# A rare loop moved ahead of the slots' layout, and the loads and the bias of a count-matrix layer reordered, in a four-layer graph network

## The chip, the cores and the metric

The kernel runs on one core of a Trainium2 chip. The core has five engines: TensorE (PE, with PEld for its weight loads), VectorE (DVE), ScalarE (ACT), GpSimd (POOL) and SyncE (SP, which mostly issues transfers). Transfers are issued from SP, ACT or POOL and are moved by 16 DMA engines. The metric is the device time of one execution in microseconds (us), the median of several. Fewer is better.

## The reference: what is computed

The input is a graph with N = 3125 nodes of 128 features and E = 100000 edges sorted by destination. Each edge has a relation (of 500), a type (of 8) and three attributes; each node has one of four types. Four layers follow one another, each with a residual and a layer norm:

```python
x = _layernorm(x + _L0_gnn_ref(x, ...))   # attention with relations
x = _layernorm(x + _L1_gnn_ref(x, ...))   # mean over the neighbours, two products
x = _layernorm(x + _L2_gnn_ref(x, ...))   # attention with an edge bias
x = _layernorm(x + _L3_gnn_ref(x, ...))   # attention with node and edge types
```

Layer 0 is a softmax over each node's incoming edges; the logits are `leaky(hP1[dst] + hP2[src] + zP3[edge_type]) @ y_w`, with eight heads. Layer 1 is

```python
summed = segment_sum(x[col], row); agg = summed / max(deg, 1)[:, None]
h = relu(agg @ W1.T + b1); return h @ W2.T + b2
```

Layer 2 adds `edge_attr @ We` (four heads) to its logits; this sum over the three attributes is the `bias` of the kernel.

## The kernel before, in words

The nodes are sorted by their number of edges and cut into 25 tiles of 128. Tile t gives every node CAP[t] slots, one for an edge, so that there are NS = 821 slots in each of 128 partitions. A node with more edges than slots is rare; its remaining edges are left to a loop, whose trips are computed on the chip (`rounds`, L476 to 488) and which makes none for these inputs.

The span has these stages.

- **Edge tables and order, 0 to 142 us.** The tables h_tab and z_tab, the table of edges and the sorted order of the nodes are made.
- **Slots' layout, L497 to 532, 142 to 193 us, in a pool of its own (`srcp`).** POOL gathers the 25 blocks of edge records into pay_sb (L503). DVE writes from them the slots' sources (srcx), masks and relations (rel). SP stores pay_sb into pay_tab (L504), for later layers, and PE, ACT and SP transpose the relations and store them as rel_tab (L529 to 532).
- **Layer 0, L885 on, 197 to 2528 us.** Its pools (`l0` and others) are opened where srcp was closed. First come m, l and nosum (L891 to 896), set to constants by DVE, and a store of nosum's zeros over sums_tab (2.4 MB, L898). Then the rare loop: `behind(wp, behind0)` calls the function at L773, which makes cur and left (L776 to 778), reads rounds into a register of every engine (L779) and runs the loop (L780). Its body `behind0` goes over all 25 tiles. After it, a planner places every step of the main work (gathers of hs rows by srcx, matmuls, softmax, sums and counts) by costs and due times; the order on DVE, ACT and PE is then as written. POOL's order (x and hs gathers) and SP's are set by the scheduler. The counts of edges between tiles are stored as c_tab, for layer 1.
- **Layer 1, L1438 to 1571, 2530 to 2730 us.** u1 (2.46 MB, L1443) holds layer 0's result times W1 in three parts of bf16. A branch (L1456, `tc.If`) deals with rare cases and is not taken here. POOL gathers 25 blocks of xn (the nodes' residual rows, in tile order). DVE makes `degrow` by way of a transpose and a transfer (L1526 to 1530). SP loads `pays` (L1536), DVE copies idx3 (L1537) and makes `bias` in twelve instructions (L1540). Then the loop over c, seven parts of 512 columns, loads the count part cs (3.2 MB, two buffers, L1546). PE adds b1 times degrow (L1549) and 75 matmuls (L1552) into y_ps. DVE and ACT make hT of it (L1554, L1555). For each of the part's four tiles, PE multiplies by W2 (o_ps, L1559), DVE adds b2 to xn (L1560), forms y and the layer norm, and PE multiplies by the next layer's weights. The scheduler may put an instruction of later source lines ahead of earlier ones on an engine, if their data allow it.
- **Layers 2 and 3, 2746 to 5236 us.** Gathers of key and value rows on POOL, products and reductions on DVE. Each has a rare loop of the same kind ahead of it.

The two places where the source order matters for the change are these:

```python
def behind(pool, body):                                   # L773
    cur = pool.tile([P, NT], F32, name="cur", bufs=1)
    V.tensor_add(cur, od.start, caps)                     # L776
    ...
    trips = nc.values_load(rounds, min_val=0, max_val=E)  # L779
    with tc.For_i(0, trips, 1):                           # L780
```

Of the kernel before, what the change touches and what calls it, by code (L numbers as in the profile page):

```python
# [86 lines left out]
def tile_gnn(ctx, tc, a, out):  # L87
# [409 lines left out]
    with tc.tile_pool(name="srcp", bufs=1) as sp, tc.tile_pool(name="srcq", bufs=2, space=PSUM) as ps:  # L497

        pay_sb = sp.tile([P, NS, PW], I32, name="pay_sb")
        start_i = sp.tile([P, NT], I32, name="start_i")  # L500
        V.tensor_copy(start_i, od.start)
        for t in range(NT):
            gather(pay_sb[:, OFF[t]:OFF[t + 1], :].rearrange("p s w -> p (s w)"), edge_tab, start_i[:, t:t + 1])  # L503
        nc.sync.dma_start(pay_tab, pay_sb.rearrange("p s w -> p (s w)"))  # L504
        srcs = sp.tile([P, NS], I32, name="srcs")
        for t in range(NT):
            sl = slice(OFF[t], OFF[t + 1])
            V.tensor_copy(srcx[:, sl], pay_sb[:, sl, 0])
            live = sp.tile([P, max(CAP)], F32, name="live", bufs=2)
            V.tensor_scalar(live[:, :CAP[t]], slotid[:, :CAP[t]], od.deg[:, t:t + 1], None, op0=OP.is_lt)  # L510
            V.tensor_scalar(mask[:, sl], live[:, :CAP[t]], -NEG, NEG, op0=OP.mult, op1=OP.add)
            V.scalar_tensor_tensor(rel[:, sl], pay_sb[:, sl, 1], float(-PADREL), live[:, :CAP[t]],
                                   op0=OP.add, op1=OP.mult)
            V.scalar_tensor_tensor(srcs[:, sl], pay_sb[:, sl, 0], float(-NP), live[:, :CAP[t]],
                                   op0=OP.add, op1=OP.mult)
        V.tensor_scalar(rel, rel, float(PADREL), None, op0=OP.add)
        V.tensor_scalar(srcs, srcs, float(NP), None, op0=OP.add)
        digit = sp.tile([P, NS], I32, name="digit")
        V.tensor_scalar(digit, srcs, 127, None, op0=OP.bitwise_and)
        V.tensor_scalar(srclo, digit, 1.0, None, op0=OP.add)  # L520
        V.tensor_scalar(digit, srcs, 7, None, op0=OP.arith_shift_right)
        V.tensor_copy(srchi, digit)

        relf = sp.tile([P, NS], F32, name="relf")
        V.tensor_copy(relf, rel)
        for o in range(0, NS, P):
            n = min(P, NS - o)
            rps = ps.tile([P, P], F32, name="rps")
            T.transpose(rps[:n], relf[:, o:o + n], ident)  # L529
            r16 = sp.tile([P, P], F16, name="r16", bufs=2)  # L530
            A.activation(r16[:n], rps[:n], AF.Copy)
            nc.sync.dma_start(rel_tab[o:o + n], r16[:n])


# [350 lines left out]

    with tc.tile_pool(name="l0", bufs=2) as wp, tc.tile_pool(name="l0s", bufs=1) as sp, \
# [4 lines left out]
        m = sp.tile([P, NT, H], F32, name="m")  # L891
        V.memset(m, LOW)
        l = sp.tile([P, NT, H], F32, name="l")
        V.memset(l, 0.0)
        nosum = sp.tile([P, D + R], F32, name="nosum")
        V.memset(nosum, 0.0)
        sums_at = sums_tab.rearrange("(t p) d -> t p d", p=P)
        nc.sync.dma_start(sums_tab.rearrange("(t p) d -> p t d", p=P),  # L898
                          nosum.unsqueeze(1).to_broadcast([P, NT, D + R]))

        def sums_of(t):
            az = wp.tile([P, D + R], F32, name="az", bufs=4)
            nc.sync.dma_start(az, sums_at[t])
            return az[:, :D], az[:, D:], az

        def own(t):
            x = wp.tile([P, D], F32, name="x", bufs=5)
            G.memset(x, 0.0)
            gather(x, a["x"], od.ids(t), bounds_check=N - 1, oob_is_err=False)
            return x  # L910

        def prologue(x):

            yield from misc.take()
            tp = ps1.tile([P, P], F32, name="tp", tag="misc")
            T.transpose(tp, x, ident)
            yield 3
            xT = wp.tile([P, P], F32, name="xT", bufs=1)
            A.activation(xT, tp, AF.Copy)
            yield 3  # L920
            pw = ps1.tile([P, D + HC + H], F32, name="pw", tag="misc")
            T.matmul(pw, xT, w0, start=True, stop=True)
            yield 3
            hw = wp.tile([P, D + HC + H], F32, name="hw", bufs=3)
            A.activation(hw, pw, AF.Copy)
            hq = wp.tile([P, 3, D], BF16, name="hq", bufs=3)
            A.activation(hq[:, 0, :], pw[:, :D], AF.Copy)
            misc.give()
            yield 3
            hrest = wp.tile([P, D], F32, name="hrest", bufs=1)  # L930
            V.tensor_sub(hrest, hw[:, :D], hq[:, 0, :])
            yield 3
            A.activation(hq[:, 1, :], hrest, AF.Copy)
            yield 3
            V.tensor_sub(hq[:, 2, :], hrest, hq[:, 1, :])
            return hw, hq

        def argument(hq, k):

            pre = ps.tile([P, 4, P], F32, name="pre")  # L940
            for i in range(3):
                T.matmul(pre[:, :k], hq[:, i, :], identb.unsqueeze(1).to_broadcast([P, k, P]), start=(i == 0),
                         stop=False)
            return pre

        def through(pre, hs, s0, k):
            for s in range(k):
                T.matmul(pre[:, s, :], hs[:, s0 + s, :D], ident, start=False, stop=(s == k - 1))  # L948

        def logits(low, k, lg_ps):  # L950
            for s in range(k):
                T.matmul(lg_ps[:, s, :], low[:, s, :], yw8, start=True, stop=True)  # L952

        def halves(v, n, last=None):

            while n > 2:
                k = n // 2
                V.tensor_add(v[:, :k], v[:, :k], v[:, n - k:n])
                n -= k
                yield 2.5  # L960
            if n == 2:
                V.tensor_add(v[:, 0] if last is None else last, v[:, 0], v[:, 1])
                yield 2.5

        def spread(ac, hs, ex, n):

            val = hs[:, :n, D:2 * D]
            valh = val.rearrange("p s (h d) -> p s h d", h=H)
            V.tensor_tensor(valh, valh, ex.unsqueeze(3).to_broadcast([P, n, H, D // H]), op=OP.mult)
            yield 2.5  # L970
            yield from halves(hs[:, :, D:2 * D], n)

        def z_rows(hs, s0, k, rl):
            zs = wp.tile([P, 4, HC + R], F32, name="zs", bufs=3)
            for s in range(k):
                gather(zs[:, s, :], z_tab, rl[:, s0 + s:s0 + s + 1])
            return zs

        def with_z(hs, s0, k, zs):
            V.tensor_add(hs[:, s0:s0 + k], hs[:, s0:s0 + k], zs[:, :k, :HC])  # L980

        def z_sums(za, zs, w):
            if len(zs) > 1:
                k = w - 4
                V.tensor_add(zs[0][:, :k, HC:], zs[0][:, :k, HC:], zs[1][:, :k, HC:])
                yield 2.5
            yield from halves(zs[0][:, :, HC:], min(w, 4))
            V.tensor_add(za, za, zs[0][:, 0, HC:])

        def drawn(steps):  # L990
            while True:
                try:
                    next(steps)
                except StopIteration as e:
                    return e.value

        up = count_up(cp, ps1.tile([P, 2 * P], BF16, name="c_up"))
        lg_at = ps1.tile([P, 2, 3 * W, H], F32, name="lg")
        misc = Room(1)

        def behind0(t, pl, mk, rl):
            _, hq = drawn(prologue(own(t)))
            ac, za, az = sums_of(t)
            lg_ps = lg_at[:, 0, :W]
            hs = wp.tile([P, W, HC], F32, name="hs", bufs=8)
            zss = []
            for s in range(W):
                gather(hs[:, s, :], h_tab, pl[:, s, 0:1])
            for s0 in range(0, W, 4):
                zss.append(z_rows(hs, s0, 4, rl))  # L1010
                with_z(hs, s0, 4, zss[-1])
            drawn(z_sums(za, zss, W))
            for s0 in range(0, W, 4):
                pre = argument(hq, 4)
                through(pre, hs, s0, 4)
                low = wp.tile([P, 4, P], F32, name="low")
                A.activation(low, pre, AF.Relu)
                logits(low, 4, lg_ps[:, s0:s0 + 4])
# [1098 lines left out]
```

## Time and profile before

| what | value |
|---|---|
| median of three runs | 5248.34 us (5230.04 to 5253.61) |
| the profiled execution | 5237.84 us, of which the span is 5236.0 us |
| mean granted PE clock in it | 0.674 of full speed |
| busy share: PE, DVE, ACT, POOL | 42%, 56%, 19%, 52% |
| POOL's gathers, hs / kv of layer 2 / kv of layer 3 | 830.3 / 781.6 / 852.5 us busy, 821 each |
| DMA | 482.23 MB, mean 92 GB/s |
| the three loads or stores that the change moves | sums_tab 2.4 MB, pays 2463 KB, cs 3200 KB each |

The page gives the busy time of each engine, the same in 40 slices of 131 us each (each digit is tenths), and the chain of work that ended last. In the timeline a row holds the start, the duration, the engine, the line, the operation and its output and input; in brackets stands how long the engine was idle before it and what released it. "SPq" and "POOLq" are the sequencers' own rows: issues of transfers, semaphores, branches.

### The profile page before, as it was taken

The page shows a single profiled execution, that of the slowest core. Times are in us where ns is not written, and L with a number is a line of the kernel's source. Part 1 is how long each engine was busy: PE and PEld are TensorE (multiplying, and loading weights), DVE is VectorE, ACT ScalarE, POOL GpSimd, SP SyncE. Part 2 cuts the span into 40 slices and gives each one's busy share as a digit, 9 for nine tenths or more (in the row PEclk, how much of TensorE's full clock was granted, in tenths as well). Part 3 has the DMA queues.
Part 4 walks back from the last instruction along what each step waited for, and adds up shares of the span by engine and source line. Part 5 has one row for each costly group of instructions (what it writes and reads, how often), then busy time and mean ns, then how long its engine had stood idle before and what let it go on. Part 6 is the DMA issues. An engine that isn't in the chain of part 4 may idle for free. (4 is left out here: it accounts for less than half of the span.)

```text
span 5236.0 us, 41120 instructions
## 1 busy us (share of the span) xinstructions
PE 2202.4 (42%) x12631; PEld 1450.8 (28%) x12631; DVE 2941.6 (56%) x6913; ACT 999.5 (19%) x2533; POOL 2723.1 (52%) x2802
## 2 busy tenths in 40 slices
PE   7176777786765777778480022322333000000000
PEld 5154455554544555555230011111111000000000
DVE  8355565665564665665524456556665455554555
ACT  1132233232322333332110011111112000000000
POOL 0524445435334443442217766666662777777774
PEclk9588788788777787888695555555556555555555
DMA  3422233323223222232343333333332333333331
GB/s 83 123 57 78 75 87 87 83 64 91 71 61 89 79 81 79 80 89 73 142 150 105 97 99 104 112 109 114 114 113 86 105 98 93 93 92 93 92 93 50
DMA packets 211921, 482.23 MB, mean 92 GB/s; under 512 B 60713, under 2 KB 110684, under 8 KB 207049
## 3 DMA queue, kind: packets, MB, share of 16 engines
q0 software_dynamic: 130688, 377.49, 25.5%
q1 hardware_dynamic: 80968, 101.69, 6.2%
q8 instruction: 106, 1.74, 0.1%
q14 instruction: 159, 1.30, 0.1%
HBM read 408.43 MB, written 70.63 MB: 91 GB/s over the span
## 5 line engine op out<-in xcount | busy, mean ns | idle before, releaser
L101 POOL DMA_INDIRECT hs<-h_tab,srcx x821 | 830.3, 1011 | 795.3 <-issue 448.8
L101 POOL DMA_INDIRECT kv<-ktv_tab,idx x821 | 852.5, 1038 | 283.2 <-issue 278.4
L101 POOL DMA_INDIRECT kv<-kv_tab,srcx x821 | 781.6, 952 | 357.5 <-issue 254.9
L1593 DVE TENSOR_TENSOR kv<-kv,qp 128x1024 f32<-128x1024 f32 (+4 forms) x228 | 253.2, 1110 | 687.2 <-DMA kv<-ktv_tab,idx 452.4
L1247 PE MATMUL zps<-oh,zq 128*128 128x512 bf16 x1472 | 415.5, 429 | 83.8 <-ACT zT L1252 40.2
L1604 DVE TENSOR_REDUCE u<-kv 128x128 f32<-128x1024 f32 (+4 forms) x228 | 383.8, 1683 | 25.1 <-issue 24.0
L1317 PE MATMUL t_ps<-zw,zT 128*128 128x136 f32 x1472 | 261.4, 315 | 147.2 <-DVE hs L1326 118.0
L1326 DVE TENSOR_TENSOR hs<-hs,t_ps 128x408 f32<-128x408 f32 (+1 forms) x276 | 145.1, 526 | 253.9 <-remote 165.5
L948 PEld LDWEIGHTS pre<-ident,hs 128*128 128x128 f32 x1642 | 244.8, 211 | 137.7 <-issue 132.7
L567 DVE TENSOR_TENSOR c_ohs<-c_ends,c_up 128x1024 bf16<-128x1024 bf16 (+3 forms) x196 | 115.9, 593 | 296.4 <-remote 207.1
L1317 PEld LDWEIGHTS t_ps<-zw,zT 128*128 128x128 f32 x1472 | 217.6, 213 | 170.6 <-issue 79.6
L1596 DVE TENSOR_REDUCE lg<-kv 128x32 f32<-128x1024 f32 (+5 forms) x228 | 251.8, 1104 | 21.7 <-issue 21.4
L948 PE MATMUL pre<-ident,hs 128*128 128x128 f32 x1642 | 250.6, 295 | 29.8 <-issue 28.5
L1600 DVE TENSOR_TENSOR kv<-kv,ex 128x1024 f32<-128x1024 f32 (+4 forms) x228 | 251.3, 1102 | 12.0 <-issue 11.9
L952 PEld LDWEIGHTS lg<-yw,low 128*128 128x128 f32 x1642 | 242.1, 222 | 42.3 <-issue 36.5
L952 PE MATMUL lg<-yw,low 128*128 128x8 f32 x1642 | 238.3, 269 | 28.9 <-issue 27.4
L677 ACT ACTIVATE c_oha<-c_oha,srclo 128x50 bf16<-128x50 bf16 (+2 forms) x821 | 213.0, 347 | 183.0 <-DVE c_oha L567 104.1
L1247 PEld LDWEIGHTS <-zq 128*128 128x128 bf16 x1472 | 157.2, 112 | 265.4 <-issue 163.6
L750 ACT ACTIVATE c_sb<-c_ps 128x512 bf16<-128x512 f32 (+1 forms) x175 | 96.3, 550 | 637.8 <-remote 332.0
L836 PE MATMUL tp<-ident,an 128*128 128x128 f32 x25 | 10.8, 434 | 480.7 <-remote 428.5
L1287 PE MATMUL pre<-zT,zw 128*128 128x512 f32 x368 | 209.3, 652 | 1.9 <-issue 1.8
L567 DVE TENSOR_TENSOR c_ohb<-c_digb,c_up 128x1024 bf16<-128x1024 bf16 (+4 forms) x123 | 73.3, 602 | 241.9 <-remote 112.5
(418 smaller groups left out, 4807.7 us busy)
## 6 DMA issues: line engine op xcount, KB each, us to landing
rb<-rel_tab SPq DMA_DIRECT2D x92, 256.0 KB
c_tab<-c_sb SPq DMA_DIRECT2D x25, 768.0 KB
cs<-c_tab SPq DMA_DIRECT2D x6, 3200.0 KB
hs<-h_tab,srcx POOLq DMA_INDIRECT x821
kv<-kv_tab,srcx POOLq DMA_INDIRECT x821
kv<-ktv_tab,idx POOLq DMA_INDIRECT x821
h_tab<-h SPq DMA_DIRECT2D x25, 132.0 KB
kv_tab<-kv SPq DMA_DIRECT2D x25, 128.0 KB
```

The lines of the kernel that those rows point to most:

```text
L101: return G.indirect_dma_start(out=dst, out_offset=None, in_=table, in_offset=indirect(idx), **kw)
L567: V.tensor_tensor(to[:, i // 2:i // 2 + k, :, :w], nums[:, i:i + k * w] .rearrange("p (b w) -> p b w", w=w).unsqueeze(2).to_broadcast([P, ...
L677: A.activation(oha[:, s // 2, 0, :, s % 2], oha[:, s // 2, 1, :, s % 2], AF.Copy, scale=srclo[:, o:o + 1])
L948: T.matmul(pre[:, s, :], hs[:, s0 + s, :D], ident, start=False, stop=(s == k - 1))
L952: T.matmul(lg_ps[:, s, :], low[:, s, :], yw8, start=True, stop=True)
L1247: T.matmul(zps, zq[:, i, 2 * R * k2:2 * R * (k2 + 1)], k.hot[i][:, cols], start=(i + k2 == 0), stop=(i == NK - 1 and k2 == 1))
L1287: T.matmul(pre[:, :n], zw[:, :D], k.zT[:, s0 * P:(s0 + n) * P], start=False, stop=False)
L1317: T.matmul(t_ps[:, s, :], k.zT[:, (s0 + s) * P:(s0 + s + 1) * P], zw[:, D:], start=True, stop=True)
L1593: V.tensor_mul(k, k, qp.unsqueeze(1).to_broadcast([P, n, D]))
L1596: V.tensor_reduce(lg, kv[:, :n, :D].rearrange("p s (h d) -> p s h d", h=heads), AX.X, OP.add)
L1600: V.tensor_tensor(v, v, ex.unsqueeze(3).to_broadcast([P, n, heads, D // heads]), op=OP.mult)
L1604: V.tensor_reduce(u, kv[:, :n, D:].rearrange("p s d -> p d s"), AX.X, OP.add)
```

## The change

It has two parts. In layer 0, m, l, nosum, the store over sums_tab, the functions that the loop's body calls (unchanged) and the loop itself now stand ahead of the slots' layout. The loop's tiles are in pools of its own (`b0`, `b0p`, `b0q`), closed before `srcp` is opened; m, l and nosum are in the pool `slots`, which is open from the start.

```diff
     rel_tab = dram.tile([-(-NS // P) * P, P], F16, name="rel_tab")
-    with tc.tile_pool(name="srcp", bufs=1) as sp, tc.tile_pool(name="srcq", bufs=2, space=PSUM) as ps:
-        pay_sb = sp.tile([P, NS, PW], I32, name="pay_sb")
...
+    m = slots.tile([P, NT, H], F32, name="m")
+    V.memset(m, LOW)
+    l = slots.tile([P, NT, H], F32, name="l")
+    V.memset(l, 0.0)
+    nosum = slots.tile([P, D + R], F32, name="nosum")
+    V.memset(nosum, 0.0)
+    sums_at = sums_tab.rearrange("(t p) d -> t p d", p=P)
+    nc.sync.dma_start(sums_tab.rearrange("(t p) d -> p t d", p=P),
+                      nosum.unsqueeze(1).to_broadcast([P, NT, D + R]))
+    with tc.tile_pool(name="b0", bufs=2) as wp, tc.tile_pool(name="b0p", bufs=2, space=PSUM) as ps, \
+            tc.tile_pool(name="b0q", bufs=1, space=PSUM) as ps1:
+        lg_at = ps1.tile([P, 2, 3 * W, H], F32, name="lg")
+        misc = Room(1)
+        behind(wp, behind0)
+
+    with tc.tile_pool(name="srcp", bufs=1) as sp, tc.tile_pool(name="srcq", bufs=2, space=PSUM) as ps:
+        pay_sb = sp.tile([P, NS, PW], I32, name="pay_sb")
...
     with tc.tile_pool(name="l0", bufs=2) as wp, tc.tile_pool(name="l0s", bufs=1) as sp, \
...
-        m = sp.tile([P, NT, H], F32, name="m")
...
         up = count_up(cp, ps1.tile([P, 2 * P], BF16, name="c_up"))
         lg_at = ps1.tile([P, 2, 3 * W, H], F32, name="lg")
         misc = Room(1)
-        behind(wp, behind0)
```

In layer 1, the loads of the first two count parts are issued by the scalar engine, and the load of pays, idx3 and the twelve bias instructions stand in the loop behind the matmuls of part 1.

```diff
-        with tc.tile_pool(name="l1pay", bufs=1) as pp:
-            pays = pp.tile([P, NS, PW], I32, name="pays")
-            nc.sync.dma_start(pays.rearrange("p s w -> p (s w)"), pay_tab)
-            V.tensor_copy(idx3, pays[:, :, 2])
-            ...
         for c in range(NCW):
             w = min(CW, NP - c * CW)
             cs = wp.tile([P, NT, CW], BF16, name="cs")
-            nc.sync.dma_start(cs[:, :, :w], ...)
+            load_by = nc.scalar if c < 2 else nc.sync
+            load_by.dma_start(cs[:, :, :w], ...)
             y_ps = ps1.tile([P, CW], F32, name="y_ps", bufs=2)
 
             T.matmul(y_ps[:, :w], b1, degrow[:, c * CW:c * CW + w], start=True, stop=False)
             for t in range(NT):
                 for k in range(3):
                     T.matmul(y_ps[:, :w], u1[:, t, k, :], cs[:, t, :w], start=False, stop=(t == NT - 1 and k == 2))
+            if c == 1:
+                with tc.tile_pool(name="l1pay", bufs=1) as pp:
+                    pays = pp.tile([P, NS, PW], I32, name="pays")
+                    nc.sync.dma_start(pays.rearrange("p s w -> p (s w)"), pay_tab)
+                    V.tensor_copy(idx3, pays[:, :, 2])
+                    for h in range(H2):
+                        for k in range(3):
+                            V.scalar_tensor_tensor(bias[:, :, h], pays.bitcast(F32)[:, :, 3 + k],
+                                                   we[:, k * H2 + h:k * H2 + h + 1], mask if k == 0 else bias[:, :, h],
+                                                   op0=OP.mult, op1=OP.add)
             hT = wp.tile([P, CW], F32, name="hT")
```

## The prediction on record

> **What bounds the kernel now.** I read the page first: the slices and the chain of work that ended last.
>
> ```profile
> POOL 0524445435334443442217766666662777777774
> POOL 15%; issue 8%; DVE 0%; another core or an unknown queue 0%; POOLq 0%; DMA 0%; DVEq 0%
> ```
>
> No engine is busy throughout, and the chain that ended last is POOL's row gathers of the last layer. That chain covers a quarter of the span, so it says nothing about the two places that the change touches: the start of layer 0 (142 to 300 us) and layer 1 (2530 to 2730 us). For these I took the table by stretches. Columns after the time: PE, PEld, DVE, ACT, POOL busy, granted PE clock, DMA share, GB/s.
>
> ```profile
> 197.00:298.00 101.00, 12.52 (x61) 7.75 (x62) 16.88 (x32) 20.12 (x64) 70.76 (x78) 0.52 0.39 106
> 298.00:340.00 42.00, 39.66 (x272) 27.80 (x272) 29.43 (x75) 11.77 (x24) 0.00 (x0) 0.93 0.08 20
> 2572.00:2602.00 30.00, 21.18 (x85) 9.04 (x84) 22.01 (x19) 0.63 (x1) 0.00 (x0) 0.78 0.48 194
> 2624.00:2730.00 106.00, 100.74 (x487) 47.97 (x485) 34.99 (x153) 19.00 (x69) 20.45 (x21) 0.99 0.41 147
> ```
>
> The reader should see two things. From 197 to 298 us only POOL is busy: 78 gathers at about 1.25 us (0.95 busy and 0.30 between) take the 100 us, and the other engines start in earnest at 298. So layer 0 begins when POOL begins, and a shift of POOL's first gather shifts the layer. From 2624 on PE is busy 100.7 of 106 us, so layer 1 ends a fixed time after PE's first free run. Then the timeline at the rare loop (L780, no trip here):
>
> ```profile
> 192.94 0.19 DVE L776 TENSOR_TENSOR cur<-start_d,caps 128x25 f32<-128x25 f32 x1 [3.20 <-DMA rel_tab<-r]
> 196.94 0.20 POOL L908 MEMSET x<- 128x128 f32 x1 [21.41 <-SPq L780]
> 197.66 0.95 POOL L101 DMA_INDIRECT hs<-h_tab,srcx  x1 [0.53 <-issue]
> 198.72 0.18 DVE L633 SCALAR_TENSOR_TENSOR crowd<-c_pre,crowd 128x25 f32<-128x25 f32 x1 [5.50 <-issue]
> ```
>
> POOL stands 21.4 us at the loop; its last gather of pay_sb ended at 175.5. Next, the timeline at the head of layer 1:
>
> ```profile
> 2552.94 0.33 SPq L1536 DMA_DIRECT2D pays<-pay_tab  x1
> 2553.37 0.85 SPq L1530 DMA_DIRECT2D degrow<-dT  x1
> 2554.27 1.42 SPq L1546 DMA_DIRECT2D cs<-c_tab  x2
> ...
> 2562.72 3.78 PE L1549 MATMUL y_ps<-degrow,b 1*128 1x512 f32 x4 [19.18 <-DMA degrow<-dT]
> ...
> 2571.50 1.01 PE L1552 MATMUL y_ps<-cs,u 128*128 128x512 bf16 x2 [5.01 <-DMA cs<-c_tab]
> ...
> 2593.31 6.45 DVE L1540 SCALAR_TENSOR_TENSOR bias<-pays,we,bias 128x821 f32<-128x821 f32 x4
> 2599.68 0.68 DVE L1554 TENSOR_TENSOR hT<-y_ps,sums 128x512 f32<-128x512 f32 x1
> ```
> ```profile
> 2601.08 0.80 PE L1559 MATMUL o_ps<-w2T,hT 128*128 128x128 f32 x2 [8.82 <-ACT hT L1555]
> ```
>
> PE gets its first count part at 2571.5, has finished part 0 at 2591.9, and then stands 8.8 us, because hT of part 0 is queued on DVE behind idx3 (2579.5) and twelve bias instructions (2580.3 to 2599.6).
>
> **Part A, the loop ahead of the slots' layout.** Removed: the barrier at 189.6 to 198.7. Of it, POOL loses 4.3 us (the last rel_tab store lands near 192.6, POOL is out at 196.9), DVE 5.7 (192.94 to 198.72). Added: the same barrier before the first pay_sb gather, now at 144.39. The loop reads rounds, ready today at 146.7 behind 25 small DVE instructions, a reduction, a transpose and two more reductions; without the memsets of l and nosum among them, some 0.4 us earlier. From the register load to DVE's first instruction behind the loop today takes 198.57 - 193.01 = 5.6 us. start_i (0.2 us) and the gather's start (1.1 us after start_i today) follow: 146.3 + 5.6 + 0.2 + 1.1 = 153.2, a delay of 9 us. The store of zeros into sums_tab (2.4 MB, issued 146.71, moving until about 156) would hold the loop to some 157 if it stays where it is: delay 12 to 13. I expect it early, since its tile is no longer in layer 0's memory. Queued behind the delayed gathers: the 25 gathers themselves, DVE's 100 small slot instructions, the pay_tab store, seven transposes, seven rel_tab stores and SP's rb loads behind these. All move by 9, so the last rel_tab store lands near 201.6.
>
> Where a loss turns to a gain is what POOL waits for then. Its first gather of layer 0 writes into memory that overlaps pay_sb's pool. Today's row for the nearest case is L776 above: a small tile in layer 0's pool waited 3.2 us for the last rel_tab store, although that store doesn't read it, so a new pool waits for the whole old one. By this row POOL starts at 201.9, **5 us later** than 196.9 (8 later with sums_tab in the way). The other end: POOL waits only for pay_sb's readers, which end at about 185.4 + 9 and need no barrier; then it starts near 194.5 or, with its indices alone (181 + 9), at 190: **2.5 to 7 us earlier**; with a loop shorter than today's, 12 earlier. I take +5. What this costs DVE is covered: counting waits at most 1 us longer (198.72 to about 199.6), and DVE is idle for 84 of the 101 us that follow. Hoisted memsets (three at 0.23 us) are worth under 1 us.
>
> **Part B, layer 1.** Removed from SP's queue: two issues (1.42 us together) and, more, their place behind pays. SP issued the last weight at 2541.2 and then stood until 2552.6 for memory that the branch at L1456 holds; pays, degrow and cs came out in one burst. On ACT, which is idle from 2543 to 2600 (0.6 us busy in the stretch above), the loads can go out at 2530.7 (before ACT's branch) or 2539 (behind it). Cost on ACT: 2 x 0.7 us beside nothing.
>
> Landing: cs is 128 packets of 25,600 B of some 0.98 us on 16 engines, so a part alone takes 7.9 us. Sent with u1 (2.46 MB until 2540 today), cs0 lands near 2545. But w2, b2 and the three weights are 128 small packets each, 8 per engine, and stand on SP's ring beside ACT's; if rings take turns by packet, as the gathers' 4,096 B packets and the 25,600 B ones do from 2560 to 2579 (xn's additions on DVE wait 29.4 us for gathers there), each small packet waits about 1 us for a large one until cs1 is through, near 2553. PE transposes w2 ahead of dT (2542.3 and 2543.1 today), and degrow follows. So the first matmul of part 0 comes not at 2546 but near 2558, against 2571.5: 13 us early, bounded by 2548 (nothing in the way) and 2566 (degrow still behind pays: 2562.7 plus its four matmuls). Part 0 takes 20.4 us: 2579 (2569 to 2587).
>
> One rule speaks against this part. The Trainium skill, "DMA: Bandwidth & Descriptors", section "Issuing engines are not separate DMA queues", says that transfers started by different engines share the same 16 DMA engines, and that a second issuer saves only the time of issuing. By it part B's first half would be worth SP's 1.42 us and no more; the rows say otherwise only because SP was standing still for 11 us before its burst.
>
> What is late next is hT of part 0 on DVE. The additions to xn must wait for 25 gathers (issued to 2566.8 by POOL whatever happens, landed by 2579.3 today, by about 2568 if cs0 and cs1 are out of the way). In program order bias now follows part 1's matmuls, but the order on DVE is the scheduler's: all 25 additions, which belong to parts 0 to 6, were already put ahead of the first hT. By this row bias (20.2 us with idx3's copy) also stays ahead if pays is early: 2568 + 21 = 2589, **10.5 us early**. If it goes behind, hT follows PE at 2579: **20 us early**, and bias then fits into DVE's idle 71 of 106 us. Ends: 2570 (30 early) and 2603 (3 late: pays and gathers crowded by cs). I take 10.
>
> What follows, layers 2 and 3, is moved as a block: nothing in them is touched, and bias is done long before 2730 either way.
>
> **Sum:** +5 - 10 = -5 us. Against the profiled execution's own 5237.84 us (span 5236.0 and 1.8 around it) that is 5233. This execution lies 10.5 us below the median of 5248.34, inside the runs' spread (5230.04 to 5253.61). I take the mean of these four times, 5242, as the level: **5237 us**.
>
> **The rivals.**
> 1. Likeliest: loop costs 5, layer 1 gives 10: 5237. For it: L776's wait and the additions hoisted ahead of hT. Chance 0.45.
> 2. Bias really goes behind hT: -20 + 5 = -15, 5227. For it: the source order; against it: DVE is free from 2568, as it was free for the additions. Chance 0.25.
> 3. POOL isn't held by the old pool either: -10 in layer 0 and -20 in layer 1, 5212. For it: POOL stood 21.4 us and needs only srcx; against it: L776. Chance 0.15.
> 4. The other side, slower: the moved barrier. It now lies on the only path to layer 0 (loop, pay_sb, rel_tab, first gather), and with the sums_tab store in front of it takes 12 us there, of which only 4.3 come back: +8, and the reload of POOL behind the loop (2.7 us for POOL's branch at L1456, 2544.85 to 2547.45) makes 11. It decides if layer 1 gives less than that, which it does when the scheduler leaves DVE's order and cs crowds the gathers: 5253. Chance 0.15, this one including that the change doesn't do what it says (the same order on all engines: 5242).
>
> Differences within 0.5% (26 us) can't be told from no change here. Under 5222 lie most of case 3 and a tail of case 2: faster 0.17. Above 5274.6 only a tail of case 4: slower 0.05. The range from 5210 to 5258 leaves out the far half of case 3 and a tail of case 4.
>
> **What the changed profile would show.** Right: a first pay_sb gather at 152 to 155, POOL's first x or hs gather at 200 to 204 with a wait on rel_tab or the pool before it, no L780 row near 195; first cs matmul at 2551 to 2562 and hT of part 0 near 2589 after the bias rows (shift layer 0's 5 us off first). Wrong: hs gathers before 195; bias rows behind the first hT; or cs rows crowding degrow so that the first matmul isn't earlier.

## The result and the profile after

The changed kernel takes 5259.34 us (median of 20 runs) against 5240.6 us for the kernel before (20 runs beside them): ratio 1.0026, 95% interval 1.0013 to 1.0038, about 14 us slower (7 to 20). The forecast was 5 us faster, 5237 us on the level of the runs then shown. The two can hardly be told apart by one run each; with 20 the sign is clear. The profiled execution took 5251.06 us, its span 5249.3 us, 13.3 us above that of before.

The page of the changed kernel looks like the one before; the chain still ends in POOL's gathers of the last layer.

```profile
POOL 0434454434334443343217756666662777777774
POOL 15%; issue 8%; DVE 0%; another core or an unknown queue 0%; POOLq 0%; DMA 0%; DVEq 0%
```

The table by stretches, moved with the stages (columns as in the prediction: PE, PEld, DVE, ACT, POOL, PE clock, DMA share, GB/s):

```profile
209.40:310.40 101.00, 12.51 (x59) 7.83 (x60) 11.76 (x27) 20.13 (x64) 69.53 (x76) 0.50 0.40 108
310.40:352.40 42.00, 37.55 (x264) 26.68 (x264) 27.48 (x67) 11.76 (x24) 0.00 (x0) 0.90 0.06 15
2572.00:2613.00 41.00, 20.65 (x78) 8.55 (x79) 25.40 (x36) 0.00 (x0) 10.82 (x11) 0.68 0.23 80
2635.30:2730.00 94.70, 94.70 (x449) 44.40 (x450) 30.45 (x131) 15.77 (x56) 15.51 (x16) 1.00 0.44 157
```

Layer 0 begins in the same manner, 12 us later: a hundred microseconds of gathers, then work on all engines. The end of layer 1 is the same stretch of TensorE work, later too. The row of 2572 to 2613 is new: TensorE, which should be in part 0 by then, is busy half of it, and POOL still gathers.

The timeline around the loop and POOL's first gather of layer 0, changed kernel:

```profile
150.82 0.13 DVE L488 TENSOR_SCALAR rounds<-rounds 1x1 int32<-1x1 int32 x1
156.80 0.18 DVE L991 CAST start_i<-start_d 128x25 int32<-128x25 f32 x1 [5.84 <-issue]
157.87 1.13 POOL L101 DMA_INDIRECT pay_sb<-edge_table,start_i  x1 [11.39 <-PE tp L798]
...
203.89 0.18 PE L592 MATMUL c_pre<-c_cnt,upperb 128*128 128x25 bf16 x1 [5.39 <-DVE c_cnt L588]
203.91 0.18 PE L593 MATMUL c_pre<-c_cnt,onesb 128*128 128x25 bf16 x1
...
203.94 0.67 PE L1019 MATMUL rps<-ident,relf 128*128 128x128 f32 x2
...
208.75 0.20 POOL L855 MEMSET x<- 128x128 f32 x1 [4.18 <-DMA rel_tab<-r]
```

The 5.84 us ahead of start_i are the loop. The first pay_sb gather, at 144.39 before, is at 157.87. And POOL, released by the last rel_tab store, starts at 208.75 instead of 196.94: 11.8 us late. Between them stands something new: three of the seven transposes of the relations (rps) run only after c_pre, a matmul of the counting that waits for VectorE until 203.9.

The head of layer 1, changed kernel:

```profile
2540.97 7.80 ACTq L1543 DMA_DIRECT2D cs<-c_tab  x2
...
2570.60 0.45 PE L798 MATMUL tp<-ident,w 128*128 128x128 f32 x1 [32.62 <-DMA wqkv<-in_L_gnn_Wv]
2570.97 2.92 DVE L1567 TENSOR_TENSOR xn<-xn,b 128x128 f32<-128x128 f32 x14 [21.61 <-DMA b<-in_L_gnn_b]
...
2572.89 0.33 SPq L1553 DMA_DIRECT2D pays<-pay_tab  x1
...
2588.94 0.88 DVE L1554 COPY idx<-pays 128x821 int32<-128x821 int32 x1
2589.74 0.27 DVE L1533 COPY dT<-dT_ps 25x128 f32<-25x128 f32 x1
...
2590.03 0.85 SPq L1535 DMA_DIRECT2D degrow<-dT  x1
...
2594.35 18.42 PE L1549 MATMUL y_ps<-cs,u 128*128 128x512 bf16 x75
...
2602.76 6.64 DVE L1557 SCALAR_TENSOR_TENSOR bias<-pays,we,bias 128x821 f32<-128x821 f32 x4
...
2612.81 0.69 DVE L1561 TENSOR_TENSOR hT<-y_ps,sums 128x512 f32<-128x512 f32 x1 [3.41 <-PE y_ps L1549]
```

The count parts go out first, at 2540.97, right behind layer 0. W2 and b2 (64 KB each), issued 2 to 3 us later, are first used at 2570.6 (the transpose by L798) and 2571.0. dT, ready on TensorE at 2571.8, is copied at 2589.7, behind all 25 additions and idx3. The twelve bias instructions follow dT, and hT of part 0 stands behind them as before; but by now it waits for TensorE, 3.4 us longer. The first count matmul is 53.4 us after the layer's first load (2540.95); before, it was 41.5 us (2571.50 - 2530.02).

### The profile page after: what moved, and what is told of

Read it like the earlier page. It is cut to its first block, busy times and chain, and to the rows that moved or that the text cites. A ratio compares the mean times of both kernels' runs of the same rounds, so it can differ in the third digit from the quotient of the medians.

```text
span 5249.3 us, 41121 instructions
## 1 busy us (share of the span) xinstructions
PE 2192.2 (42%) x12631; PEld 1443.2 (27%) x12631; DVE 2942.7 (56%) x6913; ACT 999.2 (19%) x2533; POOL 2719.2 (52%) x2802
## 5 line engine op out<-in xcount | busy, mean ns | idle before, releaser
L529 DVE TENSOR_TENSOR c_ohs<-c_ends,c_up 128x1024 bf16<-128x1024 bf16 (+3 forms) x196 | 115.7, 592 | 285.1 <-remote 193.1
L899 PE MATMUL lg<-yw,low 128*128 128x8 f32 x1642 | 233.4, 266 | 29.4 <-issue 27.7
L798 PE MATMUL tp<-ident,an 128*128 128x128 f32 x25 | 11.0, 438 | 518.4 <-remote 448.9
```

The costliest lines, as they stand in the source:

```text
L529: V.tensor_tensor(to[:, i // 2:i // 2 + k, :, :w], nums[:, i:i + k * w] .rearrange("p (b w) -> p b w", w=w).unsqueeze(2).to_broadcast([P, ...
```

## The experiments

Each comparison has its ratio to the kernel before, run beside it. One caution first. In all thirteen profiles the main part of layer 0 is the same work, yet the time from POOL's first memset there to layer 1's first load lies anywhere between 2306 and 2344 us. So a single span says little about an edit worth 10 us; the tables below compare places inside a stage, and the ratios come from repeated runs.

**Part A alone**: the loop and what belongs to it moved, layer 1 as before.

> Part A alone (loop, m, l, nosum and the store over sums_tab ahead of the slots' layout; layer 1 as before). Theory: the loss of the whole change is part A's, made of 4.0 us at the head (the order of the nodes is ready at 146.3 instead of 142.3, because the store over sums_tab is issued at 8.3 us ahead of dst's loads), 9.5 us for the barrier in front of the first pay_sb gather, less 1.7 us given back before POOL's first gather of layer 0. So that gather at 207 to 211 against 197.7, the first load of layer 1 10 to 12 us late, the total +9 to +13 us. Rival: the 4 us at the head are chance from one execution to the next, and the whole is +5 to +8.

Ratio 1.0035, interval 1.0016 to 1.0054: 8 to 28 us slower, where I expected 9 to 13. POOL's first gather of layer 0 comes at 209.6, as expected. The first load of layer 1 is only 7.4 us late in this profile instead of 10 to 12, because layer 0 happened to take 4.6 us less than in the profile of before.

**Part B alone**: layer 1 as changed, the loop where it was.

> Part B alone (layer 1 as changed, loop where it was). Theory: the two loads on the scalar engine's queue crowd out the small transfers (W2 lands 27 us after its issue) and DVE's copy of dT stands behind all 25 additions and idx3, so that the first matmul of part 0 comes 12 us later than before and hT of part 0 2 us later: total 0 to +4 us. Rival: layer 1 loses only because layer 0 ends in another state; alone the part gains: hT of part 0 near 2589, -10 us.

Ratio 0.9991, interval 0.9973 to 1.001: no difference. The loss of the whole change is part A's, and part B's gain is missing.

**Only the bias moved**: layer 1 as changed, but with all count parts loaded by SP, and the loop where it was.

```diff
-            load_by = nc.scalar if c < 2 else nc.sync
-            load_by.dma_start(cs[:, :, :w], ...)
+            nc.sync.dma_start(cs[:, :, :w], ...)
```

> Only the bias moved behind the matmuls of part 1; all count parts loaded by SP as before. Theory: without the second queue cs of part 0 goes out right behind the weights (near 2541.5), lands near 2550, degrow behind it; dT stays early on DVE and hT of part 0 stands ahead of all but two of the bias instructions: first matmul of part 0 at 2550 to 2556, hT of part 0 at 2571 to 2580, total -18 to -28 us. Rival: the gathers of xn hold DVE until 2579 whatever the order, and bias then fills in: -5 to -10 us.

Ratio 0.997, interval 0.9952 to 0.9987: faster, by about 16 us (7 to 25), a little under the 18 to 28 that I expected. In its timeline SP sends cs of part 0 right behind the weights, degrow next, and pays late:

```profile
2550.80 1.30 SPq L1537 DMA_DIRECT2D cs<-c_tab  x1
...
2554.65 0.86 SPq L1530 DMA_DIRECT2D degrow<-dT  x1
...
2566.97 18.22 PE L1543 MATMUL y_ps<-cs,u 128*128 128x512 bf16 x75
...
2573.58 0.32 SPq L1547 DMA_DIRECT2D pays<-pay_tab  x1
2574.06 0.94 POOL L101 DMA_INDIRECT xn<-x_tab,ranki  x1 [13.22 <-DMA xn<-x_tab,ranki]
...
2590.01 3.25 DVE L1551 SCALAR_TENSOR_TENSOR bias<-pays,we,mask 128x821 f32<-128x821 f32 x2
2593.17 0.69 DVE L1555 TENSOR_TENSOR hT<-y_ps,sums 128x512 f32<-128x512 f32 x1
```

hT of part 0 now stands ahead of ten of the twelve bias instructions. TensorE begins 26.4 us after the layer's first load (2540.62). My figures were on before's clock: the first matmul at 2550 to 2556, where it is 2556.4, and hT at 2571 to 2580, where it is 2582.6, 17 us earlier than before. That hT waits longer than TensorE (through at 2585.2 in this profile) is due to the gathers: POOL stalls 13.2 us among them, and VectorE's additions follow.

**Only the two loads moved to the scalar engine's queue**, bias and loop where they were:

```diff
-            nc.sync.dma_start(cs[:, :, :w], ...)
+            load_by = nc.scalar if c < 2 else nc.sync
+            load_by.dma_start(cs[:, :, :w], ...)
```

> Only the first two count parts loaded from the scalar engine's queue; bias where it was. Theory: this edit alone does the harm: W2 lands about 25 us late, dT stands behind the 25 additions and idx3 on DVE, first matmul of part 0 at 2580 to 2586, hT of part 0 at 2599 to 2605 behind bias: 0 to +5 us. Rival: the early loads bring the first matmul forward to about 2555 and hT of part 0 to 2589: -10 us.

Ratio 1.0019, interval 0.9999 to 1.0039. W2, dT and the first matmul come within half a microsecond of where they come with the whole part B, as the table shows. So this edit alone makes the delay; whether it alone costs the total anything, the interval doesn't quite say. In the whole part B it also undoes the bias move: with it, the order on VectorE keeps all bias instructions ahead of hT, although the source has them behind.

Layer 1 by kernel, in us from its first load (that of we) to: W2's transpose read out by ACT, the dT copy, the first count matmul, hT of part 0 and of part 6, and the first gather of layer 2. The kernels without a change in layer 1 end it at 216.7 to 218.7, so about 2 us are scatter.

| kernel | W2 | dT | count matmul | hT 0 | hT 6 | layer 2 |
|---|---|---|---|---|---|---|
| before | 12.8 | 13.6 | 41.5 | 69.7 | 193.1 | 216.8 |
| after | 30.1 | 48.8 | 53.4 | 71.9 | 194.8 | 219.0 |
| part B alone | 30.2 | 48.8 | 53.5 | 72.0 | 194.9 | 218.9 |
| two loads alone | 30.2 | 49.3 | 53.9 | 72.3 | 195.2 | 219.9 |
| bias alone | 12.9 | 13.7 | 26.4 | 52.6 | 180.9 | 204.7 |
| part B, dT on ACT | 30.4 | 31.1 | 43.8 | 68.5 | 193.3 | 216.4 |
| part B, small loads first | 17.6 | 18.3 | 45.0 | 62.7 | 183.0 | 207.8 |
| bias, b2 late | 12.7 | 13.4 | 25.5 | 46.8 | 173.0 | 198.3 |
| bias, b2 late, small loads first | 7.7 | 8.5 | 25.9 | 48.2 | 175.7 | 200.3 |

**The zeros' store later**: part A alone, with nosum, its zeros and the store moved up behind the edges' loads. The zeros are now made from loaded sources, so that the store can't go out ahead of them:

```diff
-    V.memset(nosum, 0.0)
+        V.tensor_scalar(nosum, src[:, :D + R], 0.0, None, op0=OP.mult)
```

> Part A alone, but the zeros for sums_tab are made from a tile of loaded sources (times zero), so that the store over sums_tab is issued behind the edges' loads instead of at 8.3 us ahead of them. Theory: the 4 us at the head are this store's; the order of the nodes is ready at 142 to 143.5 again, the first pay_sb gather at 153.5 to 155, POOL's first gather of layer 0 near 206, total +7 to +10 us. Rival: the head stays at 146 (the loop's earlier place or the moved code costs it), or the store only hurts elsewhere in the head: nothing gained.

Ratio 1.004, interval 1.0025 to 1.0055. The head is as I expected: the order of the nodes is ready at 143.84 instead of 146.59, and POOL's first x at 206.2 instead of 208.9. In the first two lines, from part A alone, dst's loads wait behind the store; in the last two, with the edit, they go first:

```profile
8.29 0.39 SPq L979 DMA_DIRECT2D sums_tab<-nosum  x1
8.79 5.69 SPq L152 DMA_DIRECT2D dst<-in_dst  x2
```
```profile
8.29 0.86 SPq L152 DMA_DIRECT2D dst<-in_dst  x2
...
21.22 1.64 SPq L444 DMA_DIRECT2D sums_tab<-nosum  x1
```

The total didn't follow (I expected +7 to +10, the interval is 13 to 29 us): layer 0 took 7 us longer in this profile than in part A's, within its scatter. So the 3 us are shown in the head, and not as a gain of the whole.

**More buffers for the transposed relations**: part A alone with

```diff
-            r16 = sp.tile([P, P], F16, name="r16", bufs=2)
+            r16 = sp.tile([P, P], F16, name="r16", bufs=7)
```

> Part A alone, with seven buffers instead of two for the transposed relations, which lets all seven transposes stand ahead of the counting's c_pre on TensorE. Theory: with part A three of the seven transposes stand behind c_pre, which waits for VectorE until 204, and that is why only 1.7 of the barrier's time come back. Then the last rel_tab store is issued near 200.5 instead of 206.8 and POOL's first gather of layer 0 comes at 203 to 205 instead of 209.6: total +4 to +7 us. Rival: POOL waits for the counting or for other things of the old pool as well: first gather at 208 or later.

Ratio 1.0024, interval 1.0005 to 1.0044: 3 to 23 us slower than before, which includes the 4 to 7 that I expected. All seven transposes are done and sent before c_pre:

```profile
198.54 3.06 SPq L1022 DMA_DIRECT2D rel_tab<-r  x7
...
204.65 0.18 PE L592 MATMUL c_pre<-c_cnt,upperb 128*128 128x25 bf16 x1 [3.94 <-DVE c_cnt L588]
...
205.23 0.10 POOL L584 MEMSET c_end<- 128x1 f32 x1 [16.01 <-DVE c_bs L597]
...
205.93 0.21 POOL L855 MEMSET x<- 128x128 f32 x1 [0.60 <-issue]
```

POOL's first x comes 3.0 us earlier than with part A alone (205.93 against 208.91), its first hs gather at 206.6, between my 203 to 205 and the rival's 208: the transposes behind c_pre cost 3 us. For the rest the rival is right: with the store out of the way POOL waits for the counting, a memset of c_end that stands ahead of x on POOL and needs c_bs.

**No loop at all**, on the kernel before:

```diff
-        behind(wp, behind0)
```

> The kernel before without layer 0's rare loop (the surplus edges of crowded nodes are left out; there are none here). It shows what the barrier cost where it was. Theory: almost nothing, since POOL's first gather waits for the last rel_tab store anyway and, with no barrier, three transposes fall behind c_pre: first x at 195 to 198 against 196.9, total -2 to +1 us. Rival 1: the store is the only thing left, x at 193, -4 us. Rival 2: POOL isn't held by the old pool at all: x near 186, -11 us.

Ratio 1.0002, interval 0.9985 to 1.002. x comes at 195.17, where the nodes' order was 1.5 us later than in before, so the barrier cost POOL 3.3 us. Without it c_pre slips in front of three transposes here as well:

```profile
190.18 0.18 PE L630 MATMUL c_pre<-c_cnt,upperb 128*128 128x25 bf16 x1 [5.44 <-DVE c_cnt L626]
...
190.24 0.67 PE L529 MATMUL rps<-ident,relf 128*128 128x128 f32 x2
...
195.17 0.20 POOL L908 MEMSET x<- 128x128 f32 x1 [4.24 <-DMA rel_tab<-r]
```

So with this order of the transposes the barrier's place could give 3.3 us at layer 0's start, too little for the total to show. It isn't the limit: here the transposes behind c_pre take back a part of the gain, and a kernel without the loop and with seven buffers was not run. Rival 2, that POOL isn't held by the old pool, falls: POOL waits for the rel_tab store in so many words.

The start of layer 0 by kernel (us):

| kernel | order of nodes | first pay_sb gather | POOL's first x | order to x |
|---|---|---|---|---|
| before | 142.3 | 144.4 | 196.9 | 54.6 |
| after | 146.3 | 157.9 | 208.8 | 62.4 |
| part A alone | 146.6 | 158.0 | 208.9 | 62.3 |
| zeros' store later | 143.8 | 155.2 | 206.2 | 62.3 |
| more buffers | 146.5 | 158.1 | 205.9 | 59.4 |
| no loop | 143.8 | 145.9 | 195.2 | 51.4 |

**dT by the scalar engine**: part B alone with

```diff
-        V.tensor_copy(dT, dT_ps)
+        A.activation(dT, dT_ps, AF.Copy)
```

> Part B alone, with dT copied by ScalarE instead of VectorE, so that it no longer stands behind the 25 additions and idx3. Counted from the first load of layer 1 (b_alone: W2 transposed at +30, first count matmul at +53.5, hT of part 0 at +72.0; before: +41.5 and +69.7). Theory: three things end together in part B; with dT freed the first count matmul comes at +38 to +42, PE is through with part 0 at +57 to +61, and hT of part 0 still waits for the late gathers' additions and then the bias: +68 to +71, a gain of 1 to 4 us only. Rival: dT's place was the whole loss, hT of part 0 follows PE at +58 to +62, 10 us or more earlier.

Ratio 1.0006, interval 0.9989 to 1.0023. The first matmul comes 10 us earlier (+43.8; I had said 38 to 42), and hT of part 0 only 3.5 us earlier, as expected:

```profile
2561.54 0.33 SPq L1548 DMA_DIRECT2D pays<-pay_tab  x1
2561.96 0.85 SPq L1530 DMA_DIRECT2D degrow<-dT  x1
...
2573.30 18.19 PE L1544 MATMUL y_ps<-cs,u 128*128 128x512 bf16 x75
...
2577.91 0.89 DVE L1549 COPY idx<-pays 128x821 int32<-128x821 int32 x1
...
2598.08 0.72 DVE L1556 TENSOR_TENSOR hT<-y_ps,sums 128x512 f32<-128x512 f32 x1
```

With dT freed, TensorE is through at 2591.5, and the twelve bias instructions hold hT until 2598. dT's place was one of several things that end together.

**Small loads first, dT on ACT, b2 late**, on part B: W2, b1 and b2 are loaded ahead of u1, and b2 is added to y behind the product (`V.tensor_add(y, y, b2)`) instead of to xn ahead of it.

```diff
+        w2 = load(sp, a["L1_gnn_W2"], "w2")
...
         u1 = sp.tile([P, NT, 3, D], BF16, name="u1")
...
-                V.tensor_add(xn[:, j, :], xn[:, j, :], b2)
...
+                V.tensor_add(y, y, b2)
```

> Part B as changed (first two count parts from the scalar engine's queue, bias behind part 1 in the source), with W2, b1 and b2 loaded ahead of u1, dT copied by ScalarE and b2 added late. Theory: the second queue hurts only through the small transfers and what waits for them; with these out of the way the first count matmul comes at +28 to +34 behind pays and degrow, TensorE is through with part 0 at +47 to +53, all bias instructions (ahead of hT on VectorE) end near +51, hT of part 0 at +48 to +54: total -14 to -22 us. Rival: the count parts crowd out u1, pays and the gathers whatever goes first: hT of part 0 at +60 or later, -10 us at most.

Ratio 0.9981, interval 0.9963 to 0.9999. hT of part 0 at +62.7: the rival is right. Even ahead of u1, W2 took until +17.6, while the count parts ran beside it (its 128 packets went from +5.6 to +14.2); pays and degrow left SP at +32.5 and +32.9. All bias instructions again stand ahead of hT and end just there (2598.62 + 6.63 = 2605.2, hT at 2605.18); TensorE, begun at +45.0, is through with part 0 at 2605.1 too, so two things end together.

**Bias and b2 late**, count parts from SP:

> The bias moved behind the matmuls of part 1 (count parts from SP, as in the run with the bias alone), and b2 added to y behind the product with W2 instead of to xn ahead of it, so that no addition waits for a gather ahead of hT of part 0. Counted from the first load of layer 1 (before: hT of part 0 at +69.7; bias alone +52.6, where TensorE was through at +44.8). Theory: the additions waiting for the late gathers held hT of part 0; without them it waits for pays, idx3 and two bias instructions only: +45 to +49, total -15 to -25 us. Rival: the gathers hold the layer later anyway (y of tile 0 needs its row), so that it ends no earlier than with the bias alone: -10 to -14 us.

Ratio 0.9972, interval 0.9956 to 0.9988. hT of part 0 at +46.8, as expected; the layer is 6 us shorter than with the bias alone. The runs don't tell the two totals apart (16 us by the one, 15 by the other), so the second half of the rival, no more than 10 to 14 us in the total, isn't excluded.

**The same with small loads first, dT on ACT and seven buffers**:

> As the run before (bias behind part 1, b2 added late), with three more: W2, b1 and b2 loaded ahead of u1, dT copied by ScalarE, and seven buffers for the transposed relations in the slots' layout. Theory: W2 is there at +6 instead of +13, the first count matmul at +21 to +25 instead of +26.3, hT of part 0 at +43 to +47; POOL's first gather of layer 0 a microsecond or two early: total -20 to -28 us. Rival: cs of part 0 and degrow behind it set the first matmul (the count part alone takes 7.9 us from an issue behind the branch), nothing gained over the run before.

Ratio 0.9963, interval 0.9943 to 0.9982: some 19 us faster than before, and faster than the changed kernel, whose interval lies wholly above 1. W2 is there 5 us sooner, but the first matmul isn't, so the rival is right on layer 1: cs of part 0, and degrow behind it, set the start. The buffers bring POOL's first x to 51.4 us after the order, against 54.3 to 55.4 in the seven kernels with the loop's old place and two buffers. That is as much as leaving out the loop gave. Whether this differs from the run with bias and b2 alone the intervals don't say.

## Why the prediction was wrong

At the loop the wait of POOL was right, and the sum left out a cost of 3 to 4 us and expected 2.6 us too much back; the mechanism in layer 1 was wrong. Part A came out 7 us above its term (11.8 against 5) and part B 12 above its own (+2 against -10, and 2 us are layer 1's own scatter); these are the 19 us between -5 and +14. That they meet the measured 14 so closely is luck in part: layer 0 took 2333.1 us in the one profile and 2332.2 in the other, where it can differ by 38.

- **"146.3 + 5.6 + 0.2 + 1.1 = 153.2, a delay of 9 us": right.** From the order of the nodes to the first gather it was 2.1 us before and is 11.6 now, 9.5 more.
- **"I expect it early", of the zeros' store: right, but the term stood at nothing without a reason: the first failing step of part A.** It went out at 8.3 us, ahead of dst's loads, and the head ended 3 to 4 us later: three kernels with the early store have their order of nodes at 146.3 to 146.6, the others at 142.3 to 144.3.
- **"All move by 9 ... POOL starts at 201.9, 5 us later": the second failing step of part A.** What POOL waits for was right: the old pool's last store. That the seven transposes move as one block was wrong. The old barrier had also kept layer 0's first counting matmuls out of the slots' layout; without it the scheduler put them between the fourth and the fifth transpose. The last rel_tab store went out at 206.6, behind them. Of the 4.3 us that were to come back, 1.7 did. Sum: 9.5 + 3 to 4 - 1.7 = 11 to 12, measured 11.8.
- **"Each small packet waits about 1 us for a large one until cs1 is through, near 2553": right mechanism, size off.** 2553 was 23 us after the layer's first load; cs1's packets ended at 27.7, and W2 was transposed at 29.7. I had not counted for W2 that u1, ahead of it on SP's queue, takes turns with cs as well: u1's packets ended at 20.2 instead of 10.0, and W2's 128 packets then took from 19.9 to 26.4, 6.5 us instead of 0.6. The 128 large packets of one count part were through at 16.9, 2546.9 on before's clock and so within 2 us of the 2545 I had given.
- **"The first matmul of part 0 comes ... near 2558": the failing step of part B.** I took the order on VectorE from the profile of before, dT ahead of 24 additions, and didn't ask whether the earlier loads would change it. They did: dT went behind 25 additions and idx3, a wait of 18 us. With dT on ACT the first matmul is still 2 us later than before (43.8 against 41.5), since degrow leaves SP behind pays, at 32.4 instead of 23.3. In place of 13 us early, the first matmul was 12 us late.
- **"Bias ... also stays ahead if pays is early": right, and the condition mattered more than I knew.** I took 2589 for hT, 59 us after the first load; with pays at +32 and the last gather issued at +45, bias ends at +68 whatever TensorE does (with dT on ACT, TensorE is through at +61.9). In the kernel with the bias moved alone, pays goes out behind cs of part 1 and hT passes ten of the twelve.
- **Part 0 "finished at 2591.9", "20.4 us": misread.** The row goes on into part 1; the 75 matmuls of part 0 end at 2590.7, after 19.2 us. The branch that rival 4 reads as 2.7 us is 2.6 by its own two times. Neither changes the result.
- **The rivals.** Rival 4 came nearest. Layer 1 gave nothing for the reason named there (cs crowds the small transfers; VectorE's order keeps the bias in front). Its 11 us at the first gather are those of the runs, but by luck: the store that it puts in front of the loop was elsewhere, and POOL's first gather behind the loop came 1.1 us after start_i, as before, so there was nothing to reload. I gave it 0.15. Rival 3 falls by the run without a loop.

The Trainium skill's rule weighed in the prediction ("DMA: Bandwidth & Descriptors", section "Issuing engines are not separate DMA queues") holds in its first half: the transfers started by ACT and SP interleave, and u1 ended 10 us later for it. Its second half, that a second issuer saves only the time of issuing, is not enough for this trace, since SP stood still: from ACT cs of part 0 was issued at +0.0 us and the first 128 of the large packets were through at +16.9, from SP at +24.3 and +40.4. But the first matmul needs W2, dT and degrow too, and these came so late that it gained nothing. And the same page, "DMA: Bandwidth & Descriptors", section "Queues, rings and completion order", says that an engine takes turns between the queues it has work for, a packet from each; I knew the turns from the gathers, and the packets of the changed kernel show them for u1 and W2 (here a packet of the trace is a single row of a transfer). Count and mean duration in stretches of 4 us, SP's queue beside ACT's:

```
2552-2556  SP: 19200 B x 38 (0.75 us)   ACT: 25600 B x 33 (0.97 us)
2556-2560  SP: 19200 B x 41 (0.75 us)   ACT: 25600 B x 32 (0.95 us)
2560-2564  SP:   512 B x 37 (0.03 us)   ACT: 25600 B x 56 (0.98 us)
2564-2568  SP:   512 B x 246 (0.03 us)  ACT: 25600 B x 44 (0.99 us)
2568-2572  SP:   512 B x 358 (0.03 us)  ACT: none
```

Until 2560 u1 and cs alternate. From 2560 to 2564 only 37 packets of 512 B, 0.03 us of work each, go through beside 56 large ones; as ACT's queue runs empty (its last packet ends at 2568.7), SP's small packets run through by the hundred. In the kernel before, 506 packets of 512 B went through in the 4 us from 2538 to 2542.

Why POOL ran late belongs here too. Its xn gathers share the turns, and in the changed kernel it waits 9.6 us in six places for gathers to finish. Its own jump over the branch at L1461 stands behind the fourteenth gather: it came at 2568.86, 27.9 us after the layer's first load, against 14.8 before (2544.85). SP's pays waits for POOL to be past it: in both profiles it goes out 0.8 us after POOL's last semaphore instruction of the branch (2552.13 and 2552.94 before, 2572.08 and 2572.89 after). So pays went from +22.9 to +31.9, and idx3 and bias with it.

## What to carry to other kernels

A loop of no trips is a barrier in these kernels (3.3 us at its old place, 9.5 at the new one), and a barrier is also a fence for the scheduler: before moving one, list what it kept apart, and price what it holds at the new place by the chain that begins there. Giving big transfers a second queue gets them out sooner when the first queue stands still, but every transfer on the first queue then takes turns with their large packets: here u1 ended 10 us later and W2 17. Look at what waits for those. Here SP's own queue did better once pays stood behind the count parts: the first matmul came at 26.4 us instead of 53.4. An order that the scheduler chose in the old program is no evidence for the new one once a load has moved.

## What the runs showed of the hardware

The main part of layer 0 (granted clock 0.81 to 0.82 between 300 and 2500 us) took 2306 to 2344 us in thirteen executions of the same work, layer 2 from its first gather to that of layer 3 took 1270 to 1278 us, and layer 3 took 1215.1 to 1215.3 us in twelve of them and 1216.2 in one. So most of the scatter of this kernel's runs, 5209 to 5254 for the kernel before, can come from layer 0, and a change outside it is better read in its own stage. Why layer 0 scatters I didn't try to find out.

Part 0's 75 matmuls took 18.4 us in the changed kernel, at a mean granted clock of 0.89, and 19.2 before, at 0.85.
